# Scan tiles of 32 channels by 4 states in a four-layer image network: sums of two steps in four column quarters, convolutions split five taps to four, one product with C on each of two engines

## The chip, the cores and the metric

The kernel runs on one core of a Trainium2 chip. A core has five engines that run side by side and wait for one another through semaphores: TensorE (PE in the profile) for matrix products, VectorE (DVE), ScalarE (ACT), GpSimd (POOL), and SyncE (SP), which here only issues transfers. ACT also issues some. The metric is the time of one execution on the device, in microseconds (us). Everything is computed in float32.

## The reference

An input of 8 images, 64 channels, 64 by 64 pixels passes four layers.

- Layer 0: full attention of every pixel on every pixel of an image (4096 by 4096 scores), then a depthwise 3x3 convolution, normalisation, a 1x1 convolution and a residual.
- Layer 1: two Swin blocks, windows of 8 by 8 pixels, 8 heads, each with an MLP.
- Layer 2: a dynamic 3x3 filter per pixel and channel, then a 1x9 convolution.
- Layer 3: a selective scan (Mamba, "SS2D") over the 4096 pixels in 4 directions k, with 128 channels and 16 states, and a pooling pyramid behind it (SAFM). Its source is a depthwise 3x3 convolution with 128 channels.

The scan is the core of layer 3. For every image, direction, channel c and state n it runs along the pixels t:

```
h = h * exp(dt[c,t] * A[c,n]) + dt[c,t] * u[c,t] * B[n,t]
y[c,t] = sum over n of h[c,n,t] * C[n,t]
```

The pyramid splits the 64 channels into four groups of 16; each is max-pooled (by 1, 2, 4, 8), convolved depthwise, enlarged again, and all are mixed by a 64x64 matrix, passed through GELU, multiplied by the input and added.

## The kernel before, in words

**Pairs and rounds.** Images are worked on in four pairs, two images of 64 channels on 128 partitions. `front(p)` does layers 0 to 2 and the scan's sources of pair p (`layer0`, `layer1`, `layer2`, `scan_sources`); `scans(p)` runs the selective scan of the pair; `back(p)` does what follows it (output norm, projection, pyramid). The first front runs alone. After that `scans(p, beside, cost)` is a loop over scan steps into which a generator `beside` is woven: for p = 0 `front(1)`; for p = 1 and 2 `back(p-1)` and then `front(p+1)`; for p = 3 `back(2)`, and towards its end `back(3)` (`late`). The generators yield costs; after each step the loop draws as much from `beside` as keeps it level with the share of steps done. These costs are constants in the code. A scheduler then sets the order of the instructions on each engine, and each engine runs its list in order. `behind(m, after)` asks for an order without a semaphore.

**A scan step.** The scan of a pair has 64 units (2 images, 4 directions, 8 chunks of 512 pixels) of 8 steps: 512 steps a round. A tile of the scan has 128 partitions: 64 channels by GRP = 2 states. One step takes two states for all 128 channels, in two column blocks j of 512 pixels, block j holding the channels 64j to 64j+63. Per unit:
- `load` brings the source, `inputs` makes dt (PE, three ACT operations) and the B and C rows (PE, ACT), and writes the rows to DRAM; `spread` multiplies dt by u and, with one DMA per channel block, lays dt and dt*u out on partitions (channel, state): `du`.
- `fetch` brings two rows of B and, separately, of C, each spread to 64 partitions, 256 KB a load, B three steps and C two steps ahead, into four buffers each.
- `products` (L1809) multiplies B by dt*u for both blocks at once on POOL, two steps ahead, into one of eight `v` tiles.
- `step`: for each block ACT makes the decay exp(dt*A) into a PSUM tile `dad` (L1831), DVE runs the recurrence along the pixels (`tensor_tensor_scan`, L1834) into an SBUF tile `hd` or back into `dad`, and ACT copies the last column to `carries` for the next chunk (L1842). Then h is multiplied by C into `v`. `own` says how many of the two products DVE does (L1848); the others go to POOL, and with own = 0 both in one instruction (L1845). Beside attention (`self.dense`) and in the last pair own is 1, and 2 at every fourth step; otherwise it is 0 at even and 1 at odd steps.
- `sums` (L1860): PE adds the two states of each channel. `fold` is a 128x64 matrix of ones and zeros; block j goes to the output partitions 64j to 64j+63 (`HALF`), that is to one half of PE's columns. Eight steps accumulate in one PSUM tile `yd`, of which there is one. `DUE` says which steps' sums are issued at which step. Each float32 matrix product stands in the profile as two MATMUL records, so a step's sums are four.
- `gather` adds `yd` to the image sum Y on DVE (L1873, L1875, L1878).

**Depthwise convolutions.** `taps_sum` (L1275, L1277) does n of the nine taps on PE, each as a product with a diagonal matrix that `spread_taps` makes, and the rest on DVE onto the PSUM tile. While the first front runs alone (`self.alone`) n is 5, beside the scan it is 9. It serves `layer0` (tile `cacc`) and `scan_sources` (tile `xacc`). In `back`, beside a scan, the first pyramid level's nine taps and the mixing matrix are one set of nine full products (tile `pa`), with the bias folded into the mixing's bias; at the very end (`alone` there) DVE does the nine taps (`sacc`, L1264).

## Time and profile before

| | us |
|---|---|
| runs | 11924.33, 11923.68, 11909.10 |
| median | 11923.68 |
| the profiled execution | 11912.44 |
| its span, first to last instruction | 11910.6 |
| first front alone | 0 to about 1578 |
| rounds 1, 2, 3 | about 1578 to 4090, to 6940, to 9790 |
| last scan and last back | about 9790 to 11911 |

The profile is of one execution. "Busy" is the time in which an engine had an instruction under way; matrix products overlap in PE's pipeline, so busy PE time is an upper measure of its work. The bounds of the rounds are the times at which the lines of one layer give way to those of the next in the trace; round 1 begins with the attention of the second image pair, and the `back` of a pair stands at the head of the round after it. In the window views each row is a stretch of the span with the busy time of each engine in it and the number of instructions; the last columns are the clock that TensorE was granted, the DMA engines' busy share and the GB/s.

The granted clock averaged 0.904.

### The profile page before, as it was taken

The page shows a single profiled execution, that of the slowest core. Times are in us where ns is not written, and L with a number is a line of the kernel's source. Part 1 is how long each engine was busy: PE and PEld are TensorE (multiplying, and loading weights), DVE is VectorE, ACT ScalarE, POOL GpSimd, SP SyncE. Part 2 cuts the span into 40 slices and gives each one's busy share as a digit, 9 for nine tenths or more (in the row PEclk, how much of TensorE's full clock was granted, in tenths as well). Part 3 has the DMA queues.
Part 4 walks back from the last instruction along what each step waited for, and adds up shares of the span by engine and source line. Part 5 has one row for each costly group of instructions (what it writes and reads, how often), then busy time and mean ns, then how long its engine had stood idle before and what let it go on. Part 6 is the DMA issues. An engine that isn't in the chain of part 4 may idle for free. (4 is left out here: it accounts for less than half of the span.)

```text
span 11910.6 us, 161652 instructions
## 1 busy us (share of the span) xinstructions
PE 9941.2 (83%) x56180; PEld 3381.8 (28%) x56180; DVE 7896.1 (66%) x9071; ACT 6958.5 (58%) x16089; POOL 7344.5 (62%) x3799
## 2 busy tenths in 40 slices
PE   9987999998889779999888968999888886665565
PEld 2244332223332223223342313222333221111111
DVE  0033368876776475876766564777676648989998
ACT  5555367766664555775665554777566355555554
POOL 0000068876777574776756673777676658889994
PEclk9998999999999889999999979999999987786768
DMA  0000055554444453554433453555343346666663
GB/s 20 1 2 2 33 168 174 172 159 120 125 131 125 152 158 111 169 170 133 132 107 110 141 177 96 157 167 173 115 132 114 109 149 190 182 191 199 207 204 119
DMA packets 779774, 1577.05 MB, mean 132 GB/s; under 512 B 89280, under 2 KB 89408, under 8 KB 778176
## 3 DMA queue, kind: packets, MB, share of 16 engines
q1 hardware_dynamic: 736320, 1443.18, 39.9%
q10 hardware_dynamic: 42624, 123.44, 3.7%
q8 instruction: 444, 7.27, 0.3%
q14 instruction: 386, 3.16, 0.1%
HBM read 1197.16 MB, written 100.66 MB: 109 GB/s over the span
## 5 line engine op out<-in xcount | busy, mean ns | idle before, releaser
L1809 POOL TENSOR_TENSOR vd<-B,du 128x1024 f32<-128x1024 f32 x2048 | 4791.4, 2359 | 2982.0 <-DMA B<-rows 1733.3
L1860 PE MATMUL yd<-vd,pack 128*64 128x512 f32 x8192 | 2707.2, 690 | 637.7 <-POOL vd L1848 505.3
L1831 ACT ACTIVATE dad<-du,As 128x512 f32<-128x512 f32 x4096 | 2716.3, 682 | 708.8 <-DVE hd L1834 330.4
L1834 DVE TENSOR_TENSOR_SCAN hd<-dad,carry,vd 128x512 f32<-128x512 f32 x1874 | 2355.3, 1270 | 529.3 <-ACT dad L1831 400.0
L1834 DVE TENSOR_TENSOR_SCAN dad<-dad,carry,vd 128x512 f32<-128x512 f32 x1710 | 2153.0, 1277 | 186.4 <-ACT dad L1831 183.4
L1848 POOL TENSOR_TENSOR vd<-hd,C 128x512 f32<-128x512 f32 x1333 | 1698.1, 1278 | 651.6 <-DVE hd L1834 648.5
L1324 PE MATMUL s<-X 64*128 64x512 f32 x4096 | 1539.3, 646 | 75.4 <-ACT e L1330 66.8
L1330 ACT ACTIVATE e<-s 128x512 f32<-128x512 f32 x2048 | 1196.3, 588 | 483.7 <-PE s L1324 483.4
L1845 POOL TENSOR_TENSOR vd<-hd,C 128x1024 f32<-128x1024 f32 x404 | 952.2, 2357 | 794.2 <-issue 393.6
L1848 DVE TENSOR_TENSOR vd<-dad,C 128x512 f32<-128x512 f32 x1955 | 1296.6, 676 | 148.5 <-ACT carry L1842 115.1
L1860 PEld LDWEIGHTS yd<-vd,pack 128*64 128x64 f32 x8192 | 643.2, 151 | 2319.1 <-issue 1129.8
L1316 PE MATMUL po<-e,VT 128*64 128x512 f32 x4096 | 1259.4, 622 | 5.8 <-ACT e L1330 5.0
L1324 PEld LDWEIGHTS s<-X 64*128 64x128 f32 x4096 | 421.8, 186 | 1178.7 <-issue 832.5
L1842 ACT ACTIVATE carry<-dad 128x1 f32<-128x1 f32 x1707 | 286.4, 169 | 760.2 <-DVE dad L1834 656.7
L1842 ACT ACTIVATE carry<-hd 128x1 f32<-128x1 f32 (+1 forms) x1521 | 302.0, 200 | 625.2 <-DVE hd L1834 611.5
L1483 PE MATMUL w_av<-wide,vals 64*32 64x64 f32 x16384 | 490.7, 225 | 117.9 <-DVE w_oc L1512 74.6
L1316 PEld LDWEIGHTS po<-e,VT 128*64 128x64 f32 x4096 | 249.6, 135 | 833.7 <-issue 569.4
L1471 ACT ACTIVATE wide<-wide 128x512 f32<-128x512 f32 x512 | 310.7, 628 | 289.4 <-DVE wide L1470 289.2
L1483 PEld LDWEIGHTS w_av<-wide,vals 64*32 64x32 f32 x16384 | 402.7, 111 | 257.1 <-issue 138.1
L1834 DVE TENSOR_TENSOR_SCAN hd<-dad,vd 128x512 f32<-128x512 f32 x267 | 319.9, 1211 | 225.6 <-POOL vd L1809 189.0
L1494 PE MATMUL w_av<-wide,each 64*32 64x128 f32 x8192 | 463.2, 280 | 5.6 <-issue 5.4
L1243 PE MATMUL pv<-n_sq,pack 128*128 128x512 f32 x576 | 345.5, 683 | 143.9 <-ACT n_sq L1241 133.3
(259 smaller groups left out, 11257.1 us busy)
## 6 DMA issues: line engine op xcount, KB each, us to landing
B<-rows SPq DMA_DIRECT2D x2048, 256.0 KB, 3.6
C<-rows SPq DMA_DIRECT2D x2048, 256.0 KB, 3.5
du<-du SPq DMA_DIRECT2D x384, 512.0 KB, 5.6
du<-du ACTq DMA_DIRECT2D x128, 512.0 KB, 5.1
xs<-xt SPq DMA_DIRECT2D x128, 256.0 KB, 3.7
xs<-xc SPq DMA_DIRECT2D x128, 256.0 KB, 3.8
xc<-xcv ACTq DMA_DIRECT2D x64, 256.0 KB, 2.0
xt<-XT ACTq DMA_DIRECT2D x32, 512.0 KB, 4.8
```

What stands on the lines that cost most here:

```text
L1316: nc.tensor.matmul(po[half[im]], lhsT=VT[:, t, half[im]], rhs=es[im], start=(t == 0), stop=(t == 31))
L1324: nc.tensor.matmul(ss[im], lhsT=at(half[im], t), rhs=X[half[im], jc * CH : (jc + 1) * CH], start=True, stop=True)
L1330: nc.scalar.activation(e, ss[im], AF.Exp, scale=C**-0.5, accum_out=parts[:, im, t, jc : jc + 1])
L1483: nc.tensor.matmul(self.av[rows, 0, x % 4 + j], lhsT=net.vals[half[im], x + j, 4 * g + h], rhs=es[g][half[im], j, h], tile_position=(64 * ...
L1494: nc.tensor.matmul(self.av[rows, 1, x % 4 : x % 4 + 2], lhsT=net.each[half[im], 32 - HD - HD * h : 64 - HD - HD * h], rhs=es[g][half[im], ...
L1809: self.nc.gpsimd.tensor_tensor(v, self.twice(st["B"]), self.units[i // 8]["du"][:, :, 1], ALU.mult)
L1831: nc.scalar.activation(da, u["du"][:, j, 0], AF.Exp, scale=net.As[:, k, n : n + 1])
L1834: nc.vector.tensor_tensor_scan(along(to), along(da), along(v[:, j]), first, ALU.mult, ALU.add)
L1842: nc.scalar.activation(cs, ends, AF.Copy)
L1845: st["w"] = nc.gpsimd.tensor_tensor(v, h, self.twice(CC), ALU.mult)
L1848: m = engine.tensor_tensor(v[:, j], hs[j], CC, ALU.mult)
L1860: m = nc.tensor.matmul(u["y"][self.HALF[j]], lhsT=w["fold"], rhs=st["v"][:, j], start=(i % 8 == 0), stop=(i % 8 == 7))
```

## The change

The scan's tile becomes 32 channels by GRP = 4 states. A step still takes two column blocks, now of 32 channels each, and four states; an even and an odd step together cover 128 channels and four states. `du` holds four blocks (16 KB a partition instead of 8), filled by four DMAs a unit instead of two. `fetch` brings four rows for two steps at once, at even steps only, into three buffers of B and three of C. `v` has seven buffers instead of eight; the `hd` tiles are three single ones instead of two double and two single.

`sums` runs once for two steps, at every odd step for the pair before: four products with a 128x32 `fold`, each to its own 32 output partitions. `DUE` goes.

`own` is 1 everywhere, so POOL and DVE do one product with C each, but for the steps with own = 2 beside attention and in the last pair, which stay. L1845, both products in one, is gone, and each block has its own carry copy.

`taps_sum` is called with n = 5 everywhere: four taps go to DVE beside the scan too. In `back` beside a scan DVE does the bias and the first four taps into an SBUF tile S (in `big`), PE the other five as full products, and one more product mixes S in. Some tiles share memory that had their own: four `e` tiles in attention instead of five, `w_h` uses the buffer of `n_sq`, `d2` that of `q2`, one `S` at the end instead of two.

```diff
-GRP = 2
+GRP = 4
...
-                        e = wk.tile([P, CH], F32, name="e", tag="e", bufs=5)
+                        e = wk.tile([P, CH], F32, name="e", tag="e", bufs=4)
...
-            diag = self.spread_taps(wk, w["dw2"])
+            diag = self.spread_taps(wk, w["dw2"], n=5)
...
-                yield from self.taps_sum(acc, diag, att, 8 * c, 1.56, wt=w["dw2"], n=5 if self.alone else TAPS)
+                yield from self.taps_sum(acc, diag, att, 8 * c, 1.56, wt=w["dw2"], n=5)
...
-        H = wk.tile([P, CH], F32, name="w_h", tag="w_h", bufs=1)
+        H = wk.tile([P, CH], F32, name="w_h", tag="n_sq", bufs=1)
...
-                    yield from self.taps_sum(acc, diag, pad, 8 * c, 1.5, wt=w["cw"], n=5 if self.alone else TAPS)
+                    yield from self.taps_sum(acc, diag, pad, 8 * c, 1.5, wt=w["cw"], n=5)
...
-                for j in self.DUE[i % 8]:
-                    if i + j >= 0:
-                        self.sums(i + j, steps[i + j], steps[i]["w"])
+                if i % 2 and i > 2:
+                    self.sums(i - 3, steps, steps[i]["w"])
...
-    def fetch(self, i, st, s):
-        n = NST * s + 2 * (i % 8)
-        t = st["BC"[s]] = self.sw.tile([P, TD], F32, name="BC"[s], tag="BC"[s], bufs=4)
-        row = self.units[i // 8]["rows"][n : n + 2]
-        self.nc.sync.dma_start(t, row.unsqueeze(0).to_broadcast([64, 2, TD]))
+    def fetch(self, i, steps, s):
+        if i % 2:
+            return
+        n = NST * s + GRP * (i % 8 // 2)
+        t = steps[i]["BC"[s]] = steps[i + 1]["BC"[s]] = self.sw.tile([P, TD], F32, name="BC"[s], tag="BC"[s], bufs=3)
+        row = self.units[i // 8]["rows"][n : n + GRP]
+        self.nc.sync.dma_start(t, row.unsqueeze(0).to_broadcast([P // GRP, GRP, TD]))
...
-        v = st["v"] = self.sw.tile([P, 2, TD], F32, name="vd", tag="v", bufs=8)
-        self.nc.gpsimd.tensor_tensor(v, self.twice(st["B"]), self.units[i // 8]["du"][:, :, 1], ALU.mult)
+        v = st["v"] = self.sw.tile([P, 2, TD], F32, name="vd", tag="v", bufs=7)
+        g = 2 * (i % 2)
+        self.nc.gpsimd.tensor_tensor(v, self.twice(st["B"]), self.units[i // 8]["du"][:, g : g + 2, 1], ALU.mult)
...
-        own = 1 + (i % 4 == 3) if u["image"] >= B - 2 or self.dense else i % 2
+        own = 1 + (i % 4 == 3 and (u["image"] >= B - 2 or self.dense))
...
-        h = wk.tile([P, 2 - i % 2, TD], F32, name="hd", tag=f"h{i % 2}", bufs=2)
+        h = wk.tile([P, TD], F32, name="hd", tag="h", bufs=3)
...
-            if at < NTD - 1 and (own or j):
-                ends = h[:, :, 0] if rev else h[:, :, TD - 1]
-                cs = self.carries[:, n0 : n0 + 2]
-                if own:
-                    ends = to[:, 0:1] if rev else to[:, TD - 1 : TD]
-                    cs = self.carries[:, n : n + 1]
-                nc.scalar.activation(cs, ends, AF.Copy)
-        if own == 0:
-            st["w"] = nc.gpsimd.tensor_tensor(v, h, self.twice(CC), ALU.mult)
+            if at < NTD - 1:
+                ends = to[:, 0:1] if rev else to[:, TD - 1 : TD]
+                nc.scalar.activation(self.carries[:, n : n + 1], ends, AF.Copy)
...
-        for j in range(2):
-            m = nc.tensor.matmul(
-                u["y"][self.HALF[j]], lhsT=w["fold"], rhs=st["v"][:, j], start=(i % 8 == 0), stop=(i % 8 == 7)
-            )
+        m = P // GRP
+        for g in range(GRP):
+            o = nc.tensor.matmul(
+                u["y"][m * g : m * g + m],
+                lhsT=w["fold"],
+                rhs=steps[i + g // 2]["v"][:, g % 2],
+                start=(i % 8 == 0),
+                stop=(i % 8 == 6),
+            )
...
+                    S = self.img(self.share(big, 3))
                     pa = self.bank("pa", (P, 8, 64))
-                    yield from self.taps_sum(pa, near, F, 8 * c, 1.5, stop=False)
+                    for t in range(TAPS):
+                        tap = F[:, 8 * c + t // 3 : 8 * c + t // 3 + 8, t % 3 : t % 3 + 64]
+                        wt = w["mw"][:, 0, t : t + 1]
+                        if t == 0:
+                            nc.vector.tensor_scalar(S, tap, wt, w["mb"][:, 0:1], ALU.mult, ALU.add)
+                        elif t < 4:
+                            nc.vector.scalar_tensor_tensor(S, tap, wt, S, ALU.mult, ALU.add)
+                        else:
+                            nc.tensor.matmul(pa, lhsT=near[:, t], rhs=tap, start=(t == 4), stop=False)
+                        if t % 3 == 2:
+                            yield 1.5
+                    nc.tensor.matmul(pa, lhsT=w["agT"][:, 0, :], rhs=S, start=False, stop=False)
```

More of the change, by code (lines that the diff above doesn't have):

```diff
@@ L1247, in normed, with spread_taps @@
         return pc, sd
-    def spread_taps(self, wk, wt, base=None):
-        d = wk.tile([P, TAPS, P], F32, name="diag", tag="diag", bufs=1)
-        for t in range(TAPS):
+    def spread_taps(self, wk, wt, base=None, n=TAPS):
+        d = wk.tile([P, n, P], F32, name="diag", tag="diag", bufs=1)
+        for t in range(n):
             self.nc.scalar.activation(
@@ L1586, in head @@
                 nc.tensor.matmul(pv, lhsT=w["var94"], rhs=q, start=True, stop=True)
-                d = wk.tile([P, CH], F32, name="d2", tag="d2", bufs=1)
+                d = wk.tile([P, CH], F32, name="d2", tag="q2", bufs=1)
                 nc.scalar.activation(d, pv, AF.Ln, bias=net.eps[:, 3:4])
@@ L1650, in scan_sources @@
             H = self.flat("H3")
-            diag = self.spread_taps(wk, w["cw"])
+            diag = self.spread_taps(wk, w["cw"], n=5)
             for c in range(NCH):
@@ L1709, in chain @@
             yield from work
-    DUE = ((-2,), (-2,), (), (-3,), (-3, -2), (-2,), (-2,), (-2,))
     def scans(self, p, beside, cost):
@@ L1733, in scans @@
             if i + 3 < n:
-                self.fetch(i + 3, steps[i + 3], 0)
+                self.fetch(i + 3, steps, 0)
             if 0 <= i + 2 < n:
-                self.fetch(i + 2, steps[i + 2], 1)
+                self.fetch(i + 2, steps, 1)
                 self.products(i + 2, steps[i + 2])
@@ L1752, in scans @@
                 (self.load, self.inputs, self.spread)[i % 8](self.units[i // 8 + 1])
-        for i in (n - 2, n - 1):
-            self.sums(i, steps[i])
+        self.sums(n - 2, steps)
         self.gather(self.units[-1])
@@ L1830, in step @@
             da = self.bank("dad", (P, TD), "da")
-            nc.scalar.activation(da, u["du"][:, j, 0], AF.Exp, scale=net.As[:, k, n : n + 1])
+            nc.scalar.activation(da, u["du"][:, 2 * (i % 2) + j, 0], AF.Exp, scale=net.As[:, k, n : n + 1])
             first = 0.0 if at == 0 else self.carries[:, n : n + 1]
-            to = da if j >= 2 - own else h[:, j]
+            to = da if j >= 2 - own else h
             nc.vector.tensor_tensor_scan(along(to), along(da), along(v[:, j]), first, ALU.mult, ALU.add)
             hs.append(to)
-            if at < NTD - 1 and (own or j):
-                ends = h[:, :, 0] if rev else h[:, :, TD - 1]
-                cs = self.carries[:, n0 : n0 + 2]
-                if own:
-                    ends = to[:, 0:1] if rev else to[:, TD - 1 : TD]
-                    cs = self.carries[:, n : n + 1]
-                nc.scalar.activation(cs, ends, AF.Copy)
-        if own == 0:
-            st["w"] = nc.gpsimd.tensor_tensor(v, h, self.twice(CC), ALU.mult)
-        for j in range(2 if own else 0):
+            if at < NTD - 1:
+                ends = to[:, 0:1] if rev else to[:, TD - 1 : TD]
+                nc.scalar.activation(self.carries[:, n : n + 1], ends, AF.Copy)
+        for j in range(2):
             engine = nc.vector if j >= 2 - own else nc.gpsimd
@@ L1849, in step, with sums @@
             st.setdefault("w", m)
-    def sums(self, i, st, after=None):
+    def sums(self, i, steps, after=None):
         nc, w, net = self.nc, self.w, self.net
-        wk, ps = self.sw, self.ps
         u = self.units[i // 8]
-        k, c = u["k"], u["c"]
         if i % 8 == 0:
-            u["y"] = ps.tile([P, TD], F32, name="yd", tag="y", bufs=1)
-        for j in range(2):
-            m = nc.tensor.matmul(
-                u["y"][self.HALF[j]], lhsT=w["fold"], rhs=st["v"][:, j], start=(i % 8 == 0), stop=(i % 8 == 7)
-            )
-            if after is not None and j == 0:
-                net.behind(m, after)
+            u["y"] = self.ps.tile([P, TD], F32, name="yd", tag="y", bufs=1)
+        m = P // GRP
[6 more added lines that the diff above has]
+                stop=(i % 8 == 6),
+            )
+            if after is not None and g == 0:
+                net.behind(o, after)
     def gather(self, u):
@@ L1956, in back @@
                 yield 7
-            ab = w["aggr_b"]
             if not alone:
                 near = self.spread_taps(wk, w["mw"][:, 0, :], w["agT"][:, 0, :])
-                pm = self.bank("pmb")
-                nc.tensor.matmul(pm[:, 0:1], lhsT=w["agT"][:, 0, :], rhs=w["mb"][:, 0:1], start=True, stop=True)
-                ab = wk.tile([P, 1], F32, name="ab", tag="ab")
-                nc.vector.tensor_tensor(ab, pm[:, 0:1], w["aggr_b"], ALU.add)
             for c in range(NCH):
@@ L1968, in back @@
                     yield from self.dwconv(acc, F, 8 * c, 8, w["mw"][:, 0, :], w["mb"][:, 0:1])
-                    S = wk.tile([P, 8, 64], F32, name="S", tag="S", bufs=2)
+                    S = wk.tile([P, 8, 64], F32, name="S", tag="S", bufs=1)
                     nc.scalar.activation(S, acc, AF.Copy)
@@ L1985, in back @@
                     )
-                last = nc.scalar.activation(pa, pa, AF.Gelu, bias=ab)
+                last = nc.scalar.activation(pa, pa, AF.Gelu, bias=w["aggr_b"])
                 nc.vector.tensor_tensor(pa, pa, self.rows(F, c), ALU.mult)
```

## The prediction

> **What bounds the kernel now.** I read the page first: the busy shares, then the costliest groups.
>
> ```profile
> span 11910.6 us, 161652 instructions
> ...
> PE 9941.2 (83%) x56180; PEld 3381.8 (28%) x56180; DVE 7896.1 (66%) x9071; ACT 6958.5 (58%) x16089; POOL 7344.5 (62%) x3799
> ...
> L1860 PE MATMUL yd<-vd,pack 128*64 128x512 f32 x8192 | 2707.2, 690 | 637.7 <-POOL vd L1848 505.3
> ...
> L1845 POOL TENSOR_TENSOR vd<-hd,C 128x1024 f32<-128x1024 f32 x404 | 952.2, 2357 | 794.2 <-issue 393.6
> ```
>
> TensorE (PE) is the busiest, and the scan's sums (L1860) are its largest group. But the average hides stages, so I cut the span where the front's lines change: 0 to 1578 us is the first front alone; then three rounds, each a scan of one image pair beside the front of the next; from 9790 us the last scan, beside little. The busy time by stretch, columns PE, weight load, DVE, ACT, POOL, clock, DMA share:
>
> ```profile
> 1578.00:2610.00 1032.00, 996.91 (x3208) 277.22 (x3206) 855.78 (x903) 755.96 (x2139) 830.52 (x448) 0.98 0.59 175
> ...
> 4537.00:5475.00 938.00, 912.00 (x2997) 252.78 (x2996) 690.97 (x731) 672.67 (x1928) 678.22 (x365) 0.99 0.53 157
> ...
> 5636.00:6380.00 744.00, 611.37 (x8666) 280.10 (x8666) 537.26 (x669) 493.06 (x967) 522.55 (x256) 0.93 0.41 122
> ...
> 6670.00:6940.00 270.00, 235.97 (x531) 83.83 (x530) 99.38 (x108) 158.68 (x256) 120.77 (x60) 0.89 0.44 141
> ...
> 10552.00:11560.00 1008.00, 573.62 (x1296) 121.15 (x1294) 943.32 (x1009) 519.96 (x1254) 922.03 (x499) 0.69 0.66 202
> ```
>
> Beside attention (first two rows) PE is busy 97%; beside the windows (third) 82%, with no engine full, so chains of waits count; beside the scan's source convolutions (fourth) 87%; in the last scan (fifth) DVE 94% and POOL 91% are the bound and PE is idle half the time. Over 1578 to 9790 the same view adds up to PE 7181 us (87% of 8212), DVE 5584 (68%). So PE time removed counts in the rounds, and nothing of it in the last 2120 us.
>
> The waits of the rounds say the same: POOL's product with B waits for a buffer that PE's sums hold.
>
> ```profile
> POOL vd L1809 <- PE yd L1860: 901.0, 133, 77.5
> ```
>
> **The change, part by part.** *Sums in four quarters.* What a quarter is worth is read from the timeline of PE:
>
> ```profile
> 3872.62 7.99 PE L1275 MATMUL xacc<-XI,diag 128*128 128x512 f32 x18
> ```
> ```profile
> 5017.08 1.03 PE L1860 MATMUL yd<-vd,pack 128*64 128x512 f32 x4
> 5018.04 1.13 PE L1324 MATMUL s<-X 64*128 64x512 f32 x4
> ```
> ```profile
> 9004.17 0.43 PE L1483 MATMUL w_av<-wide,vals 64*32 64x64 f32 x16
> 9004.39 0.45 PE L1494 MATMUL w_av<-wide,each 64*32 64x128 f32 x8
> ```
>
> Full-width records stream 18 x 512 columns in 7.99 us, 1153 columns a us; the sums in halves 2048 columns from 5017.08 to 5018.04, 2130 a us; the window products, four tiles in the four column quarters, 1024 columns in 0.22 us, 4650 a us. So four quarters run together. Today two steps cost 2 x 0.96 = 1.92 us; after, 8 records in fours, 4096 columns at 4650, are 0.88 us. I halve L1860. By the same window view of the tile yd its busy time in the rounds is 1923 us: 962 go. In the last scan 782 us are halved too, for nothing.
>
> *Convolutions five to four.* L1275 is 67 us in each attention-output convolution (three), 130 us in each source convolution (three), 63 us in each pooling tail (two within the rounds). Four taps of nine leave PE in the first two: 89 + 174 us; in the tail 18 records a chunk become 10 and 2, a third: 42 us. PE removed in the rounds: 962 + 305 = 1267 us. DVE gets 96 + 192 taps at 756 ns (L1277) = 218 us, and in two tails 48 taps at 752 ns (L1264) with 16 first taps at 0.80 us = 49 us.
>
> *Products with C one each.* Where both went to POOL (L1845, 395 times in the rounds, 2357 ns) POOL now does one (1278 ns) and DVE one (677 ns): POOL -426 us, DVE +267 us. Beside attention and in the last scan nothing changes here. DVE in the rounds becomes 5584 + 218 + 49 + 267 = 6118 us, above PE's 7181 - 1267 = 5914. So DVE is late next.
>
> *Moved at no cost.* ACT writes one more carry at those 395 steps (395 x 0.17 = 67 us, ACT is 40 to 72% busy). SP issues half as many B and C loads (2048 instead of 4096, 256 KB each) and, with ACT, twice as many du loads (1024 instead of 512, 512 KB): traffic falls by 256 MB of 1577. The even step waits only for the first two du loads of a unit, as now; the other two have a step more. In the last scan du is issued by ACT: 128 more issues at about 0.6 us, 77 us, on an engine 52% busy. Uncovered, they would delay the exps and so DVE; I take 10 of 0 to 77. Buffers: v 8 to 7 and the pair is summed a step later for its first half, so the product's lead falls by about two steps; the h tiles from four to three. Both cost something only if PE is late, and PE gets earlier.
>
> **Stage by stage** (before, what I take off, ends):
> - Attention, first round, 1032 us: PE 997 - 156 = 841, DVE 856, POOL 831, all three full together. The last scan holds DVE at 94%, so 856/0.936 = 915; with 20 for friction 935: -97 (-60 to -117).
> - Attention, rounds two and three, 938 and 941: PE 912 - 125 = 787, at 97% 811, plus 27 for DVE now at 83%: -100 each (-60 to -127).
> - Attention's convolution and norm, 164, 161, 162: PE loses 48, DVE goes from 85 to 117. 117/0.87 = 135; I take -22 each (0 to -48).
> - Windows and MLP, 746, 744, 740: the same work alone took 535 us (665 to 1200 us), and 535 plus the sums' 172 is 707, so the sums stand in its chain. Halved they give 86; but DVE, on the chain too, gets 43 more, and a PE less busy is granted less clock (0.93 at 82% busy here, 0.69 at 57%). -35 each (+20 to -86).
> - Layer 2, 300, 290, 290: half the sums is 27; DVE +15: -12 each (+10 to -27).
> - Scan sources, 270 each: PE 236 - 58 - 20 = 158, DVE 99 + 48 + 11 = 158; alone 149 us (1400 to 1549). -48 each (-15 to -78).
> - Two tails, 415 and 413: PE -73, DVE +50: -20 each (+30 to -73).
>
> Sum: 97 + 200 + 66 + 105 + 36 + 144 + 40 = 688 us off.
>
> *Last scan.* DVE-bound, and it gets one tail's 24 taps and 8 first taps: 24 us, while back(2) runs (9790 to 10552, DVE 87%). These taps read S and F, both in SBUF. Such an operation beside POOL is in the trace, and the same one without POOL:
>
> ```profile
> 4385.24 2.46 DVE L1922 TENSOR_TENSOR pool<-big 128x256 f32<-128x256 f32 x1
> ```
> ```profile
> 11826.52 0.42 DVE L1922 TENSOR_TENSOR pool<-big 128x256 f32<-128x256 f32 x1
> ```
>
> 2.04 us longer; POOL's product, which had started 0.6 us earlier, ends just before. At worst 32 x 2.04 = 65 us, at best none. I take 50 for taps and blocking (0 to 89), and 10 for ACT: +60.
>
> The Trainium skill (SBUF — State Buffer, "Who interferes with whom") states the rule behind those rows: a DVE instruction with two SBUF inputs and a GpSimd instruction that reads SBUF exclude each other for the whole instruction. By it, half a product of 2.36 us is lost per tap, an estimate of 28 us for 24 taps, and the POOL side waits too; without it 24 us would stand alone.
> The Trainium skill (TensorEngine Tiling (Array Packing), "Key Properties") also says that changing the tiling mode drains TensorE. Attention's products po and the sums share a mode today (128*64) and no longer will. The timeline shows starts 0.91 us apart without a change (po to yd) and 1.06 with one (s to po): 0.15 us for some 340 pairs would be 51 us over the three attention stages, inside the 74 us of friction allowed there.
>
> The profiled execution took 11912 us; the median of the runs is 11924, 0.1% more. 11912 - 688 + 60 = 11284, so I predict **11285 us**, 5.4% less.
>
> **Rivals.**
> 1. *DVE takes the bound over early.* DVE's 6118 us would have to run at 81% of the shortened rounds (8212 - 688 = 7524). The first round's attention shows 83% beside a full PE, the windows only 72%. If they reach 79%, the rounds take 7744, 468 off, and the whole 11504; at 77%, 7945, and 11705. For it: the scan chain ACT exp, DVE scan, ACT carry, with DVE one more product at every other step. Against: the last scan runs at 94%.
> 2. *Slower: the quarters don't run together.* The w_av tiles use two quarters per row half; the sums ask four streams on all 128 rows, which no row shows. One at a time, 4096 columns at 1153 a us cost 3.55 us for two steps, 1.63 more than now. Two at a time gain nothing; it decides for slower from 2.25 us for two steps, where 768 pairs x 0.33 eat the convolutions' 250. Serial: 768 pairs x 1.63 = 1250, less some 250 for the convolutions, PE-bound: 12900.
> 3. *The change does more than I take:* all 1267 us of PE are time: 10700 with the last scan's 60.
> 4. *No effect:* POOL and PE, now tied in pairs by seven buffers, wait on each other; each round keeps its length: about 11900.
>
> **How the numbers follow.** Forecast (10950 to 11500) 0.58; rival 1 0.21; rival 3 0.05; rival 4 0.06, half of it slower, a third within 0.2%; rival 2 0.10. A difference of 0.2% is about what a measurement of this kernel can tell. Faster: 0.58 + 0.21 + 0.05 + 0.01 = 0.85; same 0.02; slower 0.13. The range takes the forecast and rival 1, 0.79: 10960 to 11700.
>
> **What would show it.** L1860's successor: 8 records start within some 0.9 us in fours, busy in the rounds near 960 us. Attention of round one at about 3.65 us a step (now 1032/256 = 4.03: its window holds 1024 records of yd, four a step). L1845 gone, POOL's wait for yd far below 901 us. DVE above PE in busy share. The last scan from the end of back(2) as long as now, 3.5 us a step (1008 us, 1148 records). The prediction is wrong if sums pair off two by two, if DVE idles while PE waits for it in the windows, or if the last phase grows by more than 100 us.

## The result and the profile after

Four runs of the changed kernel took 11981.12 to 11998.69 us, median 11990.75 us; the kernel before, beside them, 11920.73 us (11909.1 to 11924.33). The ratio is 1.006, 95% interval 1.0043 to 1.0078: the change makes it 0.6% slower, where 11285 us (10960 to 11700) had been predicted.

The head of the page after and two groups (line, engine, operation, tiles, count, then busy us, mean ns, and idle time before with what ended most of it):

```profile
span 11990.0 us, 158089 instructions
...
PE 9126.8 (76%) x55454; PEld 2948.1 (25%) x55454; DVE 8400.8 (70%) x9856; ACT 7033.8 (59%) x16467; POOL 6919.4 (58%) x3799
...
L1808 POOL TENSOR_TENSOR vd<-B,du 128x1024 f32<-128x1024 f32 x2048 | 4799.1, 2361 | 3573.3 <-DMA B<-rows 1759.4
...
L1852 PE MATMUL yd<-vd,pack 128*32 128x512 f32 x8192 | 1823.0, 738 | 766.0 <-POOL vd L1841 519.3
```

DVE gained 505 us of busy time, about as foreseen (534 in the rounds and 24 in the last scan). PE lost 814, less than foreseen: 1267 in the rounds and half of 782 in the last scan had been forecast. PE, the fullest engine, is less full, DVE's share rises from 66 to 70%, and the span still grew. The stretches that answer to the five shown of before (bounds moved to where this kernel's layers change; columns as there):

```profile
1574.00:2615.00 1041.00, 917.01 (x3204) 205.91 (x3204) 859.99 (x907) 756.86 (x2151) 836.58 (x452) 0.93 0.58 141
4514.00:5425.00 911.00, 839.38 (x2985) 195.57 (x2984) 693.16 (x733) 671.40 (x1936) 668.36 (x360) 0.97 0.54 131
5602.00:6340.00 738.00, 577.43 (x8661) 276.60 (x8662) 545.95 (x702) 481.59 (x979) 420.56 (x236) 0.87 0.39 94
6637.00:6836.00 199.00, 151.08 (x335) 49.92 (x334) 117.62 (x145) 147.83 (x214) 84.01 (x47) 0.75 0.52 152
10470.00:11612.00 1142.00, 522.24 (x1330) 84.72 (x1330) 974.95 (x1044) 533.08 (x1295) 955.84 (x518) 0.61 0.58 150
```

In the first round's attention PE has 80 us less to do and the stage is no shorter (1031 before): PE's share fell from 97% to 88%, and its clock from 0.98 to 0.93. In the last scan DVE, 94% busy before, is 85% busy: 295 steps in 1142 us are 3.87 us a step, where before 286 in 1008 were 3.52. So something makes the bound engines wait, and the same view over all rounds says how much came back. Before, then after:

```profile
1578.00:9773.00 8195.00, 7228.73 (x41834) 2513.83 (x41832) 5614.43 (x6329) 5062.93 (x11775) 5596.28 (x2847) 0.94 0.47 141
```
```profile
1574.00:9619.00 8045.00, 6551.27 (x41168) 2151.66 (x41166) 6080.06 (x7075) 5155.83 (x12167) 5187.98 (x2853) 0.88 0.48 119
```

The rounds are 150 us shorter, and the last scan with its back, 2138 us before, takes 2371: +233. With 4 us less in the first front these make the 79 us that the spans differ by. Fewer bytes move (119 GB/s for 141), and yet the DMA engines are no less busy (0.48 for 0.47).

**Stage by stage**, the prediction against the profiles: the columns "after" and "after, du halved" are differences from the kernel before. A stage ends in every kernel where the first or last instruction of its layer stands, so the bounds of before differ a little from those above. The last column is an experiment told below, the change with all du loads on SP and half of them left out:

| us | predicted | after | after, du halved |
|---|---|---|---|
| attention, three | -297 | -64 | -164 |
| its convolution and norm | -66 | +57 | +53 |
| windows and MLP | -105 | -27 | -39 |
| layer 2 | -36 | -14 | -15 |
| sources | -144 | -84 | -103 |
| tails (two) | -40 | -20 | -49 |
| last scan | +60 | +233 | -46 |

What is late in the last scan is in the timeline (start, length, engine, what; in brackets the idle time before and its releaser):

```profile
10903.82 8.32 ACTq L1790 DMA_DIRECT2D du<-du  x4
...
10912.19 0.23 ACT L1837 ACTIVATE carry<-dad 128x1 f32<-128x1 f32 x2 [9.12 <-DMA du<-du]
...
10912.39 1.89 DVE L1841 TENSOR_TENSOR vd<-dad,C 128x512 f32<-128x512 f32 x3 [2.75 <-ACT carry L1837]
```

ACT issues a unit's four du loads, is held by that for 8.32 us, and the carries, exps, and then DVE wait behind it. Over the last scan ACT's time for issuing du grows from 69 us to 422. In the rounds SP is held in the same way, with the loads of B and C behind it; before, two loads let it go after 1.20 us. After, then before:

```profile
2000.14 7.28 SPq L1790 DMA_DIRECT2D du<-du  x4
2007.53 2.31 SPq L1799 DMA_DIRECT2D C<-rows  x1
```
```profile
3007.93 1.20 SPq L1794 DMA_DIRECT2D du<-du  x2
3009.78 1.41 SPq L1801 DMA_DIRECT2D C<-rows  x1
```

Around those loads the DMA engines are nearly full, by the window view (the last two columns are their share and GB/s; the mean of the stretches is 0.5 to 0.6). Two rows of after in the last scan, and one of before, around the load at 3007.93 us:

```profile
10904.00:10913.00 9.00, 3.23 (x12) 0.19 (x4) 6.25 (x6) 0.81 (x5) 8.52 (x5) 0.50 0.94 209
10913.00:10918.00 5.00, 4.16 (x12) 0.70 (x12) 5.00 (x7) 4.30 (x11) 2.39 (x2) 0.65 0.97 265
```
```profile
3013.00:3018.00 5.00, 2.55 (x25) 1.31 (x27) 5.00 (x6) 2.88 (x8) 4.23 (x3) 1.00 0.87 270
```

For these 14 us of the some 31 that a unit takes there is little room for other transfers. That is not new, but it lasts longer. Over all units, from the first issue of du to its last landing, the median share of the DMA engines was 0.88 in the rounds and 0.82 in the last scan before, and is 0.87 and 0.89 after; this stretch was 0.20 and 0.33 of a unit, and is 0.41 and 0.54. In the rounds a unit's two loads had landed 7.1 us after the first issue (median); now the first two have landed after 9.0 us and all four after 14.3. The page's list of transfers, after, then before, then with two of the four loads (KB each, median us from issue to landing):

```profile
du<-du SPq DMA_DIRECT2D x768, 512.0 KB, 8.8
...
du<-du ACTq DMA_DIRECT2D x256, 512.0 KB, 9.3
```
```profile
du<-du SPq DMA_DIRECT2D x384, 512.0 KB, 5.6
du<-du ACTq DMA_DIRECT2D x128, 512.0 KB, 5.1
```
```profile
du<-du SPq DMA_DIRECT2D x512, 512.0 KB, 7.8
```

The last line has as many loads of the same size as before, and each still takes 2 us longer to land. So the shape of a load (32 channels to 4 partitions each, not 64 to 2) may count beside their number; no run prices it alone.

### The profile page after: what moved, and what is told of

The parts are those of the page before. It is cut to its first block, busy times and chain, and to the rows that moved or that the text cites. A ratio compares the mean times of both kernels' runs of the same rounds, so it can differ in the third digit from the quotient of the medians.

```text
span 11990.0 us, 158089 instructions
## 1 busy us (share of the span) xinstructions
PE 9126.8 (76%) x55454; PEld 2948.1 (25%) x55454; DVE 8400.8 (70%) x9856; ACT 7033.8 (59%) x16467; POOL 6919.4 (58%) x3799
## 5 line engine op out<-in xcount | busy, mean ns | idle before, releaser
L1841 POOL TENSOR_TENSOR vd<-hd,C 128x512 f32<-128x512 f32 x1737 | 2207.4, 1277 | 1362.7 <-DVE hd L1833 1313.4
L1833 DVE TENSOR_TENSOR_SCAN dad<-dad,carry,vd 128x512 f32<-128x512 f32 x2064 | 2595.2, 1274 | 358.2 <-ACT dad L1830 335.4
L1852 PE MATMUL yd<-vd,pack 128*32 128x512 f32 x8192 | 1823.0, 738 | 766.0 <-POOL vd L1841 519.3
L1833 DVE TENSOR_TENSOR_SCAN hd<-dad,carry,vd 128x512 f32<-128x512 f32 x1520 | 1925.2, 1268 | 471.6 <-ACT dad L1830 269.4
L1841 DVE TENSOR_TENSOR vd<-dad,C 128x512 f32<-128x512 f32 x2359 | 1552.3, 674 | 214.9 <-ACT carry L1837 212.3
L1324 PE MATMUL s<-X 64*128 64x512 f32 x4096 | 1480.1, 656 | 68.8 <-ACT e L1330 65.8
L1316 PE MATMUL po<-e,VT 128*64 128x512 f32 x4096 | 1182.5, 635 | 14.7 <-ACT e L1330 10.9
L1852 PEld LDWEIGHTS yd<-vd,pack 128*32 128x32 f32 x8192 | 258.3, 119 | 2099.5 <-POOL vd L1841 1055.2
L1837 ACT ACTIVATE carry<-hd 128x1 f32<-128x1 f32 x1521 | 303.8, 200 | 698.4 <-DVE hd L1833 690.6
L1767 PE MATMUL pdd<-xs,xdt 128*128 128x512 f32 x512 | 374.0, 820 | 365.7 <-DVE hd L1833 229.7
```

The lines of the kernel that those rows point to most:

```text
L1316: nc.tensor.matmul(po[half[im]], lhsT=VT[:, t, half[im]], rhs=es[im], start=(t == 0), stop=(t == 31))
L1324: nc.tensor.matmul(ss[im], lhsT=at(half[im], t), rhs=X[half[im], jc * CH : (jc + 1) * CH], start=True, stop=True)
L1833: nc.vector.tensor_tensor_scan(along(to), along(da), along(v[:, j]), first, ALU.mult, ALU.add)
L1837: nc.scalar.activation(self.carries[:, n : n + 1], ends, AF.Copy)
L1841: m = engine.tensor_tensor(v[:, j], hs[j], CC, ALU.mult)
L1852: o = nc.tensor.matmul(u["y"][m * g : m * g + m], lhsT=w["fold"], rhs=steps[i + g // 2]["v"][:, g % 2], start=(i % 8 == 0), stop=(i % 8 == 6),
```

## The experiments

The theory: du's four loads a unit, 2 MB instead of 1, make the loss. The rivals: the smaller buffers, DVE's two-input taps beside POOL, and a lower value of PE's time than was taken.

**The issuer, and the volume up and down.** First, all du loads on SP, in the changed kernel:

```diff
-        queue = nc.scalar if u["image"] >= B - 2 else nc.sync
+        queue = nc.sync
```

> The changed kernel, with the du loads of the last image pair issued by SP like those of the other pairs, instead of by ACT. Theory 1 (du loads: four of 512 KB a unit fill the transfer queue, and the engine that issues them is held: ACT's issues of du grew from 124 to 474 us in the last scan): the last phase, 2358 us in the changed kernel against 2121 before, loses 100 to 240 us, so the whole is 11750 to 11890. Theory 2 (seven v buffers and paired sums make the engines wait for one another, du stands by): within 40 us of the changed kernel, 11950 to 12030. Theory 3 (DVE's taps in the tail, which have two SBUF inputs, block GpSimd): no difference either.

11859.03 us, 0.995 of before (0.9933 to 0.9966); the last scan with its back takes 2235 us instead of 2371. So 132 us of the loss are ACT's issuing.

Second, in the kernel before, each du load sent twice to the same place:

```diff
-            queue.dma_start(du...)
+            for _ in range(2):
+                queue.dma_start(du...)
```

> The kernel before, with each du load issued twice to the same place: its bytes double, as in the change, and nothing else is touched. Theory 1: 100 to 300 us slower than before, most of it in the last scan (ACT held) and some beside attention of the first round (GpSimd waiting for du). Theories 2 and 3: within 40 us of before.

12402.7 us, 1.0398 (1.0381 to 1.0416), that is 476 us slower, 420 of them in the last scan, and more than either theory had. The largest of its waits, and two groups of issues in the rounds:

```profile
POOL vd L1810 <- DMA du<-du: 1845.3, 118, 1553.7
```
```profile
2001.91 1.20 SPq L1795 DMA_DIRECT2D du<-du  x2
...
2006.64 2.88 SPq L1795 DMA_DIRECT2D du<-du  x2
```

One wait of 1553.7 us is the first front; the rest, 292 us, is twice what POOL waits for du on that line in the kernel before (144 us; 154 over all its lines). These 476 us are not the price of the volume alone. A repeat writes where the first copy writes, so it is issued only when that has landed (in the unit shown at 2006.58 and 2008.93 us, the repeats following at 2006.64 and 2009.00). In the last scan du is complete 20.8 us after its first issue (median) instead of 8.9, and ACT, which issues it there, waits 170 us for du in all instead of 7.

Third, the changed kernel on SP with two loads a unit instead of four; channels 64 to 127 of du are left out:

```diff
-        du = u["du"] = self.sw.tile([P, GRP, 2, TD], F32, name="du", tag="du")
+        du = u["du"] = self.sw.tile([P, 2, 2, TD], F32, name="du", tag="du")
-        for g in range(GRP):
+        for g in range(2):
```

> The changed kernel with du loads on SP and half of them left out: the blocks of channels 64 to 127 are not loaded, odd steps use the blocks of channels 0 to 63 again, so the sums of the scan are not the reference's. Two loads of 512 KB a unit, as before the change. Theory 1 (du volume): the last phase returns to about 2140 and GpSimd's wait for du beside attention (164 us in the first round) goes, attention there 950 to 1000: 11580 to 11720 in all. Theory 2 (seven v buffers, paired sums): within 40 us of 11859.

11546.57 us, 0.9685 (0.9668 to 0.9701): 312 us less than with four loads, a little more than forecast for du. The issue time of du on SP falls from 1895 us to 330. The attention stages take 987, 887 and 891 us.

**The time of the loads.** The changed kernel on SP, with the source loaded two units ahead and du sent one step earlier:

```diff
-            if i >= 0 and i % 8 < 3 and i // 8 + 1 < len(self.units):
-                (self.load, self.inputs, self.spread)[i % 8](self.units[i // 8 + 1])
+            if i >= 0 and i % 8 < 2 and i // 8 + 1 < len(self.units):
+                (self.inputs, self.spread)[i % 8](self.units[i // 8 + 1])
+            if i >= 0 and i % 8 == 7 and i // 8 + 2 < len(self.units):
+                self.load(self.units[i // 8 + 2])
```

> The changed kernel with du loads all on SP (as in after_du_sync, 11859 us) and the next unit's inputs and du issued one step earlier in the unit, its source loaded two steps earlier. If du comes too late (a question of lead), the last phase goes from 2235 to about 2150 and attention of the first round from 1045 to below 1000: 11700 to 11800. If it is the volume of du that holds the queue, the earlier start gains nothing: 11820 to 11890.

11715.92 us, 0.9828 (0.9812 to 0.9844). POOL's waits for du fall from 550 to 189 us. The kernel is now 1.7% faster than before, with the whole change in it. So the forecast for a question of lead (how long ahead of its use a load is sent) came in, and that for volume (11820 to 11890) did not: the same bytes, a step earlier, cost 143 us less. The last scan gains 66 of them and the two tails 70; attention gains nothing (2889 us against 2877, with some 15 scan steps more in it).

**The other parts of the change, alone.** In the kernel before: five taps on PE and four on DVE in the two convolutions; then `own` of the changed kernel; then both.

```diff
-                yield from self.taps_sum(acc, diag, pad, 8 * c, 1.5, wt=w["cw"], n=5 if self.alone else TAPS)
+                yield from self.taps_sum(acc, diag, pad, 8 * c, 1.5, wt=w["cw"], n=5)
```
```diff
-        own = 1 + (i % 4 == 3) if u["image"] >= B - 2 or self.dense else i % 2
+        own = 1 + (i % 4 == 3 and (u["image"] >= B - 2 or self.dense))
```

> The kernel before with the two depthwise convolutions of the front split five taps on PE to four on DVE beside the scan too; sums, tiles and pyramid as before. The prediction's terms without the sums' share (cacc: PE -30, DVE +24 a round; xacc: PE -58, DVE +48 a round) give 60 to 200 us faster. The rival (DVE pays back what PE gains) gives -40 to +40.

> The kernel before with one product with C on GpSimd and one on DVE at every step where both were on GpSimd; all else as before. GpSimd loses 1.08 us and DVE gains 0.68 us at 395 steps of the rounds. If GpSimd's product time was on the path in the windows stage: 30 to 100 us faster. If DVE is in the chain there, as the profile of the changed kernel suggests (GpSimd's wait for the recurrence grew from 47 to 143 us in that stage): 0 to 60 us slower.

> The kernel before with both parts that were faster alone: front convolutions five to four (measured -131 us alone) and one product with C on each engine (-93 us alone); scan tile, sums, buffers and pyramid as before. If the two relieve different engines (PE and GpSimd), they add: 11700 us, 11660 to 11740. If both lean on the same free time of DVE, they share it: 11760 to 11800.

11795.4 us (0.9893, 0.9877 to 0.991), 11833.56 us (0.9929, 0.9913 to 0.9946), and 11724.26 us together (0.9839, 0.9823 to 0.9856). Nearly additive, 131 and 93 against 195. So these parts are good. What the products with C gain lies less in the windows (15 us), where the forecast had looked for it, than in the two tails (56 us). The way from there to the changed kernel, by differences of runs: 11724 with both; 178 less for all the rest of the change (tile, sums, buffers, the tail's taps) with half its du; 312 more for the other half; 132 more for ACT's issuing: 11990. And with du a step earlier the whole change takes 11716 us: beside these two parts the four-state tile then gains 8 us, less than these runs can tell.

**Buffers.** The kernel before with seven `v` tiles instead of eight (`bufs=8` to `bufs=7`):

> The kernel before with seven v buffers instead of eight. Theory 2: GpSimd's product waits more for the sums, 50 to 150 us slower. Theory 1: 0 to 20 us slower.

11819.86 us, 0.9918 (0.9901 to 0.9934): fewer buffers were faster by some 100 us, 57 of them in the last scan. POOL's waits for du fell from 154 to 20 us. That POOL, with less lead in products, stands less often before a missing du is argued, not shown. So seven tiles don't cost in the kernel before. The other smaller buffers (`e`, `hd`, B and C) were not tried alone. In the changed kernel with du on SP and a step earlier, six tiles instead of seven took 11739.24 us (0.9848, 0.9831 to 0.9864), 23 us more; 20 to 100 less had been expected if fewer tiles help there as well, 20 to 150 more if the pairs of sums need them. POOL's waits for du fell from 189 to 32 us in it, and those for yd rose from 1032 to 1295, so the waits for du that were left did not set the time of the early kernel. Seven tiles on the two good parts (`n=5`, `own`) give the lowest time of the kernels that compute the whole:

> The kernel before with front convolutions five to four, one product with C on each engine, and seven v buffers. Seven buffers alone were 99 us faster than before, the other two together 195. If the three are independent: 11620, 11590 to 11660. If seven buffers helped only because they move GpSimd's products behind its products with C, which the second change relieves already: 11700 to 11740.

11692.26 us, 0.9814 (0.9797 to 0.983): 32 us below the two parts alone, not 99, so seven tiles mostly overlap with them. With du on SP and a step earlier too, as above:

> As before_taps_c_v7, with the du loads all on SP and the next unit's inputs and du one step earlier. If du's lead costs something in the kernel before too (GpSimd waits 144 us for du there): 20 to 120 us faster than before_taps_c_v7. If two loads of 512 KB a unit are early enough with seven buffers: within 20 us of it.

11900.64 us, 0.9985 (0.9975 to 0.9994), 208 us worse. POOL waits for du 14 us in it, 18 without; the loss is in attention (1069, 999, 997 us instead of 1019, 953, 956) and layer 2 (348, 328, 328 instead of 312, 319, 319). What the early inputs displace there stays open.

**DVE's taps.** The changed kernel with early du, and in `back` all nine taps on PE again, as before the change:

```diff
-                    for t in range(TAPS):
-                        ...
-                    nc.tensor.matmul(pa, lhsT=w["agT"][:, 0, :], rhs=S, start=False, stop=False)
+                    yield from self.taps_sum(pa, near, F, 8 * c, 1.5, stop=False)
```

> The changed kernel with du on SP and a step earlier (11716 us), with the pooling tail's nine taps all on TensorE as in the kernel before, none on DVE. If DVE's taps there cost by exclusion with POOL as the prediction feared: the last scan is 50 us shorter and the tails of the rounds gain or lose 20: -50 us (-90 to -20). If DVE has room for them: the tails get back TensorE's work of 42 us each: +10 to +80 us.

11709.69 us, 0.9822 (0.9806 to 0.9839), against 0.9828 with DVE's taps: no difference. In the profiles the last scan is 26 us shorter and each tail in the rounds some 20 longer.

**What PE's time is worth.** The kernel before, with the sums of six steps in eight left out:

```diff
-        for j in range(2):
+        for j in range(2 if i % 8 in (0, 7) else 0):
             m = nc.tensor.matmul(
```

> The kernel before with the sums of two steps in eight alone (the first and the last of a unit); the other six are left out, so the scan's output is not the reference's. It takes three quarters of the sums' PE time away, 1440 us in the rounds, more than the change can. If the sums stand in the chain of the windows stage, as the prediction has it (535 us alone plus 172 of sums), that stage goes from about 750 to about 620, and the whole to 10900 to 11200. If they only fill gaps there, it stays above 725, and the gain is beside attention (950 to about 800 in rounds two and three, 1031 to 930 in the first): 11350 to 11600.

11886.73 us, 0.9974 (0.9963 to 0.9986): three quarters of 2707 us of PE's sums bought 28 us, and neither forecast came in. The windows stage takes some 853 us instead of 752, but with more scan steps in it (172 instead of 128 in rounds two and three), and layer 2 and the sources take some 82 us a round less with fewer. Three lines of its timeline in attention, and two of its waits from 4532 to 5468 us:

```profile
4892.55 1.12 PE L1324 MATMUL s<-X 64*128 64x512 f32 x2
...
4904.35 2.35 POOL L1809 TENSOR_TENSOR vd<-B,du 128x1024 f32<-128x1024 f32 x1 [6.75 <-DMA du<-du]
...
4913.69 2.07 PE L1324 MATMUL s<-X 64*128 64x512 f32 x2
```
```profile
POOL vd L1809 <- DMA du<-du: 172.2, 22, 11.2
...
DVE vd L1848 <- DMA C<-rows: 68.5, 30, 6.9
```

Two things stand where the sums were; how much each takes back is not shown. POOL now waits 742 us for du instead of 154, 552 of them in attention: the du loads of the kernel before seem to have been just early enough for the pace that PE set. And PE, idle between its matrix products, is granted less clock: two records of scores take 2.07 us, at a granted clock of 0.50, that took 1.12 at 1.00 shortly before, and the mean is 0.831 instead of 0.904. The Trainium skill (TensorE: Matmul & The Clock Gate, Part 1) says that TensorE falls to half clock once it has been idle for long enough; these rows agree with half, and no run here shows the length of idleness that it takes.

So PE's time had to be priced where du is out of the way: the changed kernel with half the loads and early, and the same with each quarter's sum issued a second time with weights of zero.

```diff
-        for g in range(GRP):
+        for x in range(2 * GRP):
+            g = x % GRP
...
-                lhsT=w["fold"],
+                lhsT=w["fold"] if x < GRP else net.none,
```

> The changed kernel with two du loads a unit instead of four (channels 64 to 127 of du are left out, the odd steps use the blocks of the even ones), on SP, and with du sent a step earlier. Two loads alone took 11546 us, four loads a step earlier 11716. Theory A, du is all that still stands between the halved sums and time: POOL's waits for du go (327 us with two loads), attention of the first round goes from 988 to about 930 us (DVE's 857 us at 0.92), the whole run to 11380 us (11300 to 11450). Theory B, the work taken off TensorE is worth next to nothing there, because other waits and a lower clock take its place: 11546 within 60 us, though the waits for du are gone.

> The run before it, with each sum of a quarter issued twice, the second time with weights of zero, so that the output of the sums stays as it was: TensorE's work for the sums is that of the kernel before again. At 0.88 us a pair of steps that is some 676 us of TensorE work in the rounds and 225 in the last scan. Theory P of the prediction, TensorE's time in the rounds is worth 0.54 of itself (688 of 1267 us): +365 us. Theory B, it is worth next to nothing: within 60 us of the run without the second sums, with the granted clock higher in it, nearer to the 0.904 of the kernel before.

11598.14 us (0.9729, 0.9713 to 0.9745) and 11948.31 us (1.0027, 1.0015 to 1.004). The first is a miss for both theories: 52 us slower than half du not early. Attention is 105 us longer in it, though POOL's waits for du fell from 327 to 135 us; some 15 more scan steps stand in that stage, and the tails, with 19 fewer, are 48 us shorter. The second is 350 us slower than the first, near theory P's 365, with the clock at 0.894 instead of 0.863. So the halved sums are worth 350 us there: 286 in attention, 65 in layer 2 (with five more scan steps a round in it), and nothing in the windows (23 us less, with fewer steps). The rows of the second round's attention, once and then twice:

```profile
4416.00:5352.00 936.00, 881.05 (x3024) 208.88 (x3023) 721.14 (x764) 691.89 (x1960) 702.26 (x377) 0.95 0.41 102
```
```profile
4522.00:5545.00 1023.00, 947.00 (x3872) 227.18 (x3873) 705.30 (x751) 689.39 (x1947) 696.66 (x374) 0.92 0.38 92
```

PE is 94 and 93% busy, and work added to it lengthens the stage: beside attention it is the bound, once du is out of the way.

**Hold, volume or lead.** The changed kernel with early du, its four loads in four steps, one each (`spread` called at i % 8 = 1 to 4 with one block); and du split over two queues, without and with the early step:

```diff
-            queue.dma_start(du[:, g].rearrange("p q t -> p (q t)"), src)
+            (nc.sync if g < 2 else nc.scalar).dma_start(du[:, g].rearrange("p q t -> p (q t)"), src)
```

> The changed kernel with du on SP and a step earlier (11716 us), with the four du loads of a unit issued in four steps, one each, instead of all in one. If four loads in a row hold SP's queue, and the loads of B and C behind them: SP's issue time for du falls from 1948 us to under 900, the last scan is 40 to 80 us shorter, the whole 20 to 150 us. If what costs is the volume of du, wherever it stands: within 20 us of 11716.

> The changed kernel with two of a unit's four du loads issued by SP and two by ACT, in all units; the same bytes, at the same step. In the traces two loads in a row take their issuer 1.2 us and four in a row 7 to 8 us. If this hold of the issuer and of what stands behind it costs, and not the volume: each queue's issue time for du is near 330 us instead of 1895 on SP alone, POOL's waits for du fall well below 550 us, and the time goes most of the way from 11859 (all on SP) to 11546 (two loads only): 11550 to 11700 us. If the volume costs: 11800 to 11900 us, as with all on SP.

> The same two queues with du a step earlier (11716 us with all on SP). If the hold of the issuer costs: 11550 to 11680 us, and the last scan 2090 to 2110 us as with two loads, not 2169. If the volume costs: within 30 us of 11716.

11713.47 us (0.9824, 0.9808 to 0.984): no change, but no test either, since the order on SP still had three or four loads in a row, with SP's issue time for them at 1818 us. The two queues: 12249.26 us (1.0279, 1.0261 to 1.0296) and 11905.88 us (0.9988, 0.9978 to 0.9997), 390 and 190 us slower than with all loads on SP; both forecasts failed in both. The hold did shrink, from 1895 us on SP to 670 on SP and 406 on ACT; in the first run the landing stayed at 8.7 us on both queues, POOL waited 738 us for du instead of 550, and ACT 288 instead of 215. So a shorter hold of SP brought nothing here. But ACT, an engine of the scan, came in as an issuer in the rounds too, so SP's hold isn't ruled out as a part of the cause, and why ACT costs that much stays open. The Trainium skill (Trainium Kernel Development and Optimization, "Key Constraints") says that transfers of all queues share the same 16 DMA engines and that more issuers save only issue time. The issue time did fall, from 1895 us to 1076, and the loads landed no sooner (8.7 us against 8.8), which agrees; the kernel was slower all the same.

What the runs show is this. The second pair of a unit's du loads costs 312 us where du is sent as in the change, and 118 where it is sent a step earlier (11716 against 11598 us); 52 of that difference is that the kernel with half the loads got slower. ACT as the issuer costs 132 more. How the price of the second pair divides among its bytes, its late landing, the hold of SP and the shape of the loads is not separated.

## Why the prediction was wrong, point by point

- *"Moved at no cost"* is the step that failed. It counted the du loads (512 to 1024), noted that the bytes fall by 256 MB of 1577, and costed the loads at nothing because "the even step waits only for the first two du loads of a unit, as now". But these two land later than the two of before (9.0 us after the first issue instead of 7.1 in the rounds), and the other two have landed only after 14.3 us. The total of the bytes was right and the wrong measure: they left the even stream of B and C and went into a burst that lasts twice as long a share of a unit. The second pair and the issuer cost 312 + 132 = 444 of the 706 us between forecast and result. The range given for ACT's part, 0 to 77 us, came from 0.6 us an issue; four in a row held ACT 8.32 us, two a load, and what was priced as extra work on an engine half idle was a stop of the chain.
- *The other 262 us* stand in the table too (265 there, since it goes by profiles). With half of du, these parts of the forecast are still missing: 133 in attention, 119 in its convolution and norm, 66 in the windows, 62 in layer 2 and the sources; the tails and the last scan are 115 us better than forecast. The points below say what is known of them.
- *The last scan*, +60 with 10 for ACT and 50 for taps and blocking, became +233, past the 100 us that the prediction had named as a sign of being wrong. It is du's loads and their issuer: with half of them, all on SP, the stage is 46 us shorter than before. The taps cost some 26 us at most, by two profiles. The exclusion of two-input DVE operations and POOL, seen in the 2.46 us row and stated by the Trainium skill (SBUF — State Buffer, "Who interferes with whom"), did not show in the whole.
- *The quarters run together*: right. Eight records take 1.00 us to the next start at full clock, and 0.89 where their own kind follows (in the run with doubled sums). After, in attention, then before, then with doubled sums:

```profile
4963.05 1.13 PE L1324 MATMUL s<-X 64*128 64x512 f32 x4
4964.11 1.08 PE L1316 MATMUL po<-e,VT 128*64 128x512 f32 x4
...
4977.39 1.07 PE L1852 MATMUL yd<-vd,pack 128*32 128x512 f32 x8
4978.39 1.08 PE L1316 MATMUL po<-e,VT 128*64 128x512 f32 x4
4979.40 1.13 PE L1324 MATMUL s<-X 64*128 64x512 f32 x4
```
```profile
5014.15 1.03 PE L1860 MATMUL yd<-vd,pack 128*64 128x512 f32 x4
5015.11 1.13 PE L1324 MATMUL s<-X 64*128 64x512 f32 x4
5016.17 1.08 PE L1316 MATMUL po<-e,VT 128*64 128x512 f32 x4
5017.08 1.03 PE L1860 MATMUL yd<-vd,pack 128*64 128x512 f32 x4
```
```profile
5009.08 1.07 PE L1857 MATMUL yd<-vd,pack 128*32 128x512 f32 x8
5009.97 1.04 PE L1857 MATMUL yd<-vd,none 128*32 128x512 f32 x8
```

- *The drain between modes* was undersized. Before, a step is yd to s 0.96, s to po 1.06, po to yd 0.91: 2.93 us, two steps 5.86. After, two steps are twice s to po 1.06, po to the next 1.01 twice, and the sums 1.00: 5.14. A pair saves 0.72 us and not 1.04; 0.32 us of friction for some 340 pairs are 109 us over attention, where 51 had been set beside an allowance of 74. The sums' busy time in the rounds fell from 1919 us to 1151, not to some 960. The Trainium skill's rule (TensorEngine Tiling (Array Packing), "Key Properties") was the right one to hold against the change, and po to yd at 0.91 without a change of mode (before, 5016.17 to 5017.08) and 1.01 with one (after, 5054.20 to 5055.21) agrees with it.
- *PE as the bound* holds beside attention and, less surely, in layer 2 (351 us for the doubled sums in the two), not beside the windows: "the sums stand in its chain" fell, the doubled sums costing nothing there. Of PE's 1267 us some 1030 went if the busy time of the rounds is weighed with the clock (7228.73 x 0.94 - 6551.27 x 0.88, an estimate); the lower clock gave a third of that back, and 677 us of busy time remained. The allowance for the clock was made in the windows only.
- *Attention*, -97, -100 and -100, came to -64 in all: a ceiling of 0.72 x 340 = 245 us of PE, and 100 lost to du's second half. Where the other 81 went stays open: POOL still waits 327 us for du with half of it, but the run in which these waits fell to 135 us had a longer attention.
- *Its convolution and norm*, -22 each, came to +19 each: some 40 scan steps now stand in it instead of 24. The loop draws work by constant costs, so the gain moves to the neighbouring stage: with the taps alone this stage took 96 us more and the windows 102 less. A stage's end isn't the unit to count in here.
- *Sources and tails*, -84 of -144 and -20 of -40 in after, -103 and -49 with half du: right in kind. *DVE in the rounds* at 6118 us: it is 6080.
- *The products with C one each* had no saving of their own; they were worth 93 us in the kernel before. *Buffers*: seven v tiles didn't cost there, as forecast.
- None of the rivals had the mechanism. The rival "no effect" came nearest with 11900 us, for a reason (POOL and PE tied by seven buffers) for which the kernel before with seven tiles gives no support. POOL's waits for yd in the rounds, foreseen far below 901 us, are 994.

## What to carry to other kernels

Price a transfer by when it must land and by what passes at the same time, not by the total: a burst that keeps the DMA engines busy for half of a unit cost 444 us here though the bytes of the whole fell, and sending it a step earlier gave 143 of them back once ACT no longer issued it. When a wait is taken from the tightest ring, look for the ring that is next (here du, it seems, which was just in time for the pace that PE set) and price it before the gain is booked, stage by stage; and let a busy share of 97% prove itself by an experiment that adds work, since taking work away also lowers TensorE's clock. Test the parts of a change alone: two of three here were good, and with seven `v` tiles they give 11692 us, 1.9% less than before, without the four-state tile.

## What was not expected of the hardware

- Two du loads of 512 KB in a row take their issuer 1.20 us, four take 7.28 to 8.32, so the third and fourth hold it about 3 us each; in the trace this looks like an engine without work, not like a busy one.
- Leaving out some 2000 us of TensorE's sums (three quarters of 2707) changed the time by 28 us and lowered the granted clock from 0.904 to 0.831.
- One `v` buffer less made the kernel before 100 us faster, and du sent earlier, all on SP, made the four-state kernel faster (143 us) and the two-state kernel with seven tiles and the two good parts slower (208 us; there SP had not issued all of du before).
